# Transposing h and h2 by 32x32 blocks on VectorE, with DMAs inside SBUF that put the blocks in place

## The chip, the core and the metric

The kernel runs on one core of one Trainium2 chip. The metric is the device time in microseconds (us) of one execution. The kernel before was timed in three runs, and their median is what a changed kernel is held against. A profile is one more execution, taken by the hardware profiler, with a time and a span of its own.

## The reference, cut to what matters

Two layers work on a batch of 128 graphs, each with 128 nodes and 512 features. All data is float32.

```python
# x: [128, 128, 512], adj: [128, 128, 128]
# layer 0
h = relu(layernorm(x))
Xw = h @ Wv + bv
e  = leaky_relu(sj[:, None, :] + si[:, :, None] + ab)     # sj, si: Xw times the halves of aw
T  = adj * exp(e), each row divided by its sum
H  = sum over k = 0, 1, 2 of  (T^k h) @ Wk[k] + bk[k]
x  = x + relu(H)
# layer 1
h2 = relu(layernorm(x))
q, k = split(h2 @ Wqk);  v = h2 @ Wv1
w  = sum over d of q * (adj @ (k * mask)), scaled
x  = x + softmax(w over the nodes) * v
```

A product with a weight matrix needs the features of h on the partitions, since TensorE contracts over partitions. But h is computed with the nodes on the partitions. So h (for layer 0, the k = 0 term) and h2 (for layer 1) have to be transposed.

## The kernel before, in words

The 128 graphs are taken in 64 pairs (`G = 2`). A pair p passes through these steps, each of which is a function or a few lines:

- `load(p)` (L65 to L70) loads x and adj of a pair: two DMAs of SP's queue into `xg` and `ag`, with three buffers each.
- `norm0(p)` (L222) starts the load of pair p+1, if it wasn't started yet, normalizes x into `h` (`norm_relu`: statistics on VectorE, the last step L216 on ScalarE) and makes the two score columns from h with four VectorE operations (L231), whose full-size result `junk` is never read.
- `begin(p)` (L413) takes a tile `x` that will hold h, Th and T²h of the pair, transposed, and calls `transposed` for h.
- `transposed` (L234 to L240) transposes a pair's h: 8 TensorE transposes of 128x128, four into each of two PSUM tiles `pt` (L239), and then one copy of 128x512 from PSUM to SBUF on ScalarE and one on VectorE (L240).
- `attention(p)` and `t_transposed(p)` make T, T transposed and T² transposed; `propagate(p)` (L285) makes Th and T²h, transposed, with 16 TensorE instructions (L293) and four ScalarE copies (L295).
- `prepare0(p)` (L319) makes four sums of blocks of `x` on VectorE (`left_sums`, L301 to L304, 128x768 each), as Strassen's scheme with seven products wants them.
- `strassen0(p)` (L322) does layer 0's seven products (L313, 84 TensorE instructions of 256 columns), with VectorE additions between them (L332 to L347). A bank of PSUM takes a second product after VectorE has read the first: product 5 is added into the bank of product 6, once L335 has read that.
- `norm_relu` makes h2 of the pair. Its tile has one buffer, and the matmul that reads the h2 of the pair before (L383) has to be done first.
- a second call of `transposed` (L453) puts h2, transposed, into the tile `x2`, which has one buffer; L454 makes its four sums `sx2` (again L301 to L304, 128x256 each).
- `strassen1(p)` (L353) does layer 1's seven products (L313, 56 instructions of 512 columns), `aggregate(p)` the matmul with adj (L383) and a weighted sum (L386), `finish(p)` the softmax, the last addition (L409) and the store of the result (L411, SP's queue).

The loop at L427 overlaps neighbouring pairs: in round p stand `strassen0(p)`, with `begin` and `attention` of pair p+1 between its products, `propagate(p+1)`, `strassen1(p-1)`, `aggregate(p-1)`, `prepare0(p+1)`, `finish(p-1)`, the transposition of h2 of pair p with its sums, and `norm0(p+2)`.

The order in which an engine gets its instructions isn't the order of this text, though. The framework in which the kernel is written puts them in a queue for each engine at build time, by the order of the text and by when its own model of the machine finds them ready; it also writes the waits on semaphores. On the chip each queue runs strictly in order. So in the profile the statistics of `norm0(p+2)` stand ahead of `strassen1(p-1)`, and single instructions of `finish` lie between those of `norm0`. If an instruction isn't ready on the chip when its turn comes, all those behind it on its engine wait. DMAs take turns on eight semaphores; one that reads what DMAs wrote waits on each of the semaphores concerned. A wait that does not fit on an instruction is an instruction of its own (EVENT_SEMAPHORE).

Of the kernel before, what the change touches and what calls it, by code (L numbers as in the profile page):

```python
# [8 lines left out]
FP = mybir.dt.float32  # L9
# [6 lines left out]
def kernel(  # L16
# [20 lines left out]
    nc = tc.nc  # L37
    B, N, D = x.shape
    K = wk.shape[0]
    P = 128  # L40
    DC = D // P
    HC = DC // 2
    HD = D // 2
    G = 2
    NP = B // G
    EPS = 1e-5
    assert N == P and B <= P and B % G == 0 and D == 4 * P and K == 3
# [81 lines left out]
    ccol = setup.tile([P, 2], FP, name="ccol")  # L129
    for a in range(2):  # L130
        for c in range(DC):
            junk = front.tile([P, D], FP, name="junk")
            nc.vector.scalar_tensor_tensor(junk, wv0_sb[:, c, :], 1.0, aw_bc[:, a, :],
                                           op0=OP.mult, op1=OP.mult, accum_out=ucol[:, a, c:c + 1])
        pu = ps_t.tile([P, DC, P], FP, name="pt")
        for c in range(DC):
            spread(pu[:, c, :], ucol[:, a, c:c + 1])
        nc.vector.tensor_copy(u_bc[:, a, :], pu.rearrange("p c i -> p (c i)"))
        junk = front.tile([P, D], FP, name="junk")
        nc.vector.scalar_tensor_tensor(junk, bv_bc, 1.0, aw_bc[:, a, :],  # L140
                                       op0=OP.mult, op1=OP.mult, accum_out=ccol[:, a:a + 1])
    cz = const.tile([P, 1], FP, name="cz")
# [27 lines left out]
    right1 = {}  # L170
# [51 lines left out]
    def norm0(p):  # L222

        if p + 1 < NP and p + 1 not in xg:
            load(p + 1)
        h = H[p] = norm_relu(xg[p], "h", front)
        s = S[p] = small.tile([P, G, 2], FP, name="s")
        for j in range(G):
            for a in range(2):
                junk = front.tile([P, D], FP, name="junk")  # L230
                nc.vector.scalar_tensor_tensor(junk, h[:, j, :], 1.0, u_bc[:, a, :], op0=OP.mult,  # L231
                                               op1=OP.mult, accum_out=s[:, j, a:a + 1])

    def transposed(h, dst):  # L234

        for j in range(G):
            pt = ps_t.tile([P, 2, HC, P], FP, name="pt")
            for c in range(DC):
                nc.tensor.transpose(pt[:, c // HC, c % HC, :], h[:, j, c * P:(c + 1) * P], ident)  # L239
            (nc.vector.tensor_copy if j else nc.scalar.copy)(dst(j), pt)  # L240

    def attention(p):

# [41 lines left out]
    def propagate(p):  # L285

        h, tt = H.pop(p), TT.pop(p)
        for j in range(G):
            for kh in range(2):
                pt = ps_t.tile([P, HC, 2, N], FP, name="pt")  # L290
                for c in range(HC):
                    at = (kh * HC + c) * P
                    nc.tensor.matmul(pt[:, c].rearrange("p k n -> p (k n)"), h[:, j, at:at + P],  # L293
                                     tt[:, j].rearrange("p k n -> p (k n)"), start=True, stop=True)
                nc.scalar.copy(X[p][:, j, kh, 1:3].rearrange("p k c n -> p c k n"), pt)  # L295

    def left_sums(blocks, pool, name, width, bufs):

        s = pool.tile([P, 4, width], FP, name=name, bufs=bufs)
        a = [[blocks[:, j, kh] for kh in range(2)] for j in range(G)]  # L300
        nc.vector.tensor_add(s[:, 0], a[1][0], a[1][1])  # L301
        nc.vector.tensor_sub(s[:, 1], s[:, 0], a[0][0])  # L302
        nc.vector.tensor_sub(s[:, 2], a[0][0], a[1][0])
        nc.vector.tensor_sub(s[:, 3], a[0][1], s[:, 1])  # L304
        return dict(zip((5, 6, 7, 3, 1, 2, 4),
                        [s[:, 0], s[:, 1], s[:, 2], s[:, 3], a[0][0], a[0][1], a[1][1]]))

    def products(left, right, width):

        def product(bank, i, first):  # L310
            n = left[i].shape[1] // P
            for c in range(n):
                nc.tensor.matmul(bank[:, :width], left[i][:, c * P:(c + 1) * P], right[i][:, c],  # L313
                                 start=(first and c == 0), stop=(c == n - 1), skip_group_check=True)
        return product

    R0 = {i: t.rearrange("p k c o -> p (k c) o") for i, t in right0.items()}

    def prepare0(p):  # L319
        SX[p] = left_sums(X[p].rearrange("p j h k c n -> p j h (k c n)"), front, "sx", K * HD, 1)  # L320

    def strassen0(p, steps):  # L322

        product = products(SX.pop(p), R0, HD)
        X.pop(p)
        lo, hi = bsum[:, :HD], bsum[:, HD:]
        hb = X1[p] = front.tile([P, G, D], FP, name="x1", bufs=3)
        s = front.tile([P, 4, HD], FP, name="s0", bufs=1)
        ba, bb, bc = (ps_m.tile([P, D], FP, name="pm") for _ in range(3))
        a, b, c = ba[:, :HD], bb[:, :HD], bc[:, :HD]  # L330
        product(ba, 1, True)
        nc.vector.tensor_add(s[:, 0], a, hi)  # L332
        nc.vector.tensor_add(s[:, 1], a, lo)
        product(bb, 6, True)
        nc.vector.tensor_add(s[:, 2], b, s[:, 1])  # L335
        steps[0]()
# [12 lines left out]
        for j in range(G):  # L349
            nc.vector.scalar_tensor_tensor(hb[:, j, :], hb[:, j, :], 0.0, xs[:, j, :],  # L350
                                           op0=OP.max, op1=OP.add)

    def strassen1(p):  # L353

        product = products(SX2.pop(p), R1, D)
        X2.pop(p)
        yv = late["p"].tile([P, G, 2, 2, HD], FP, name="yv")
        o = [[yv[:, j, nh].rearrange("p k d -> p (k d)") for nh in range(2)] for j in range(G)]
        s = late["p"].tile([P, 3, D], FP, name="s1")
        a, b, c = (ps_m.tile([P, D], FP, name="pm") for _ in range(3))  # L360
        product(a, 1, True)
        nc.scalar.copy(s[:, 0], a)
        product(b, 6, True)
        nc.vector.tensor_add(s[:, 1], b, s[:, 0])
        product(c, 7, True)
        product(b, 5, False)
        nc.vector.tensor_add(s[:, 2], b, s[:, 0])
        nc.vector.tensor_add(o[1][1], c, s[:, 2])
        product(a, 2, False)
        nc.scalar.copy(o[0][0], a)  # L370
        product(b, 3, False)
        nc.vector.tensor_add(o[0][1], b, s[:, 0])  # L372
        product(c, 4, False)
        nc.vector.tensor_add(o[1][0], c, s[:, 1])  # L374
        return yv

    def aggregate(p, yv):

        h2, at = H2.pop(p), AT.pop(p)
        w = small.tile([P, 6, G], FP, name="w")  # L380
        for j in range(G):
            pa = ps_t.tile([P, D], FP, name="pt")
            nc.tensor.matmul(pa, at[:, j, :], h2[:, j, :], start=True, stop=True)  # L383
            junk = front.tile([P, D], FP, name="junk")
            b = p * G + j
            nc.vector.scalar_tensor_tensor(  # L386
                junk.rearrange("p (k d) -> p k d", k=2), pa.rearrange("p (k d) -> p k d", k=2),
                wscale[:, b:b + 1], yv[:, j, :, 0, :], op0=OP.mult, op1=OP.mult,
                accum_out=w[:, 0, j:j + 1])
        return w  # L390
# [20 lines left out]
        nc.sync.dma_start(out[p * G:(p + 1) * G].rearrange("b n d -> n b d"), x1)  # L411

    def begin(p):  # L413
        X[p] = front.tile([P, G, 2, K, HC, N], FP, name="x")
        transposed(H[p], lambda j: X[p][:, j, :, 0])

    nothing = (lambda: None, lambda: None)
    norm0(0)
# [6 lines left out]
    R1 = None  # L425
    W = {}
    for p in range(NP + 1):  # L427
# [9 lines left out]
        if p == 0:  # L437
            score_matrix()
            setup_ctx.close()
            R1 = {i: t.rearrange("p c k o -> p c (k o)") for i, t in right1.items()}  # L440
            late["p"] = ctx.enter_context(tc.tile_pool(name="late", bufs=1))
        if p < NP:
            H2[p] = norm_relu(X1[p], "h2", late["p"])
# [6 lines left out]
            finish(p - 1, yv, w)  # L450
        if p < NP:
            X2[p] = late["p"].tile([P, G, 2, HC, N], FP, name="x2")
            transposed(H2[p], lambda j: X2[p][:, j])  # L453
            SX2[p] = left_sums(X2[p].rearrange("p j h c n -> p j h (c n)"), late["p"], "sx2", HD, 1)  # L454
        if p + 2 < NP:
            norm0(p + 2)

# [24 lines left out]
```

## Time and profile before

| | |
|---|---|
| median of three runs | 2532.59 us (2530.12 to 2532.79) |
| the profiled execution | 2529.95 us, of which the span 2528.2 us |
| mean granted TensorE clock | 0.995 |
| busy: PE (matmul), PEld (weight load) | 2491.1 us, 1794.9 us |
| busy: DVE (VectorE), ACT (ScalarE) | 1700.4 us, 698.6 us |
| DMA moved | 86.28 MB in 62473 packets |
| one round in the steady state | 38.5 us |
| transposes of h and h2, L239 | 1024 instructions |
| copies of them to SBUF, L240 | 128 on ScalarE (586 ns each), 128 on VectorE (675 ns each) |

How to read it: the span is the time from the first to the last instruction of the profiled execution, and what the time has beyond it lies around the span. Busy times are sums over an engine's instructions in which overlaps count once. The engines run side by side, so that the busy times don't add up to the span. TensorE's matmuls overlap each other: the duration of one (273 ns for a transpose) is its latency, and the distance between two is what it costs TensorE.

### The profile page before, as it was taken

How to read it: one execution, taken by the hardware profiler on the slowest of the kernel's cores; microseconds unless marked ns; L12 is line 12 of the kernel's file. 1: busy time of each engine (PE TensorE's matmuls, PEld its weight loads, DVE VectorE, ACT ScalarE, POOL GpSimd, SP SyncE). 2: the span in 40 equal slices, each digit the busy share in tenths (PEclk: the TensorE clock that was granted, in tenths of full speed). 3: DMA queues.
4: the chain of work that ended last, by engine and by line, in shares of the span. 5: the costliest groups of instructions: out<-in, count | busy, mean ns of one | idle time of the engine just before them, and what ended most of it. 6: DMA issues, size and time to landing. Idle time of an engine off the chain costs nothing.

```text
span 2528.2 us, 28170 instructions
## 1 busy us (share of the span) xinstructions
PE 2491.1 (99%) x10313; PEld 1794.9 (71%) x10313; DVE 1700.4 (67%) x4648; ACT 698.6 (28%) x1677; POOL 0.7 (0%) x6
## 2 busy tenths in 40 slices
PE   5999999999999999999999999999999999999998
PEld 4677676776776776776767767767767767677675
DVE  6666667667667666666676676676666666766764
ACT  2322222223223223222222232232232222222321
POOL 0000000000000000000000000000000000000000
PEclk8999999999999999999999999999999999999999
DMA  5110010001000100100100010001001001000000
GB/s 161 36 38 30 28 38 29 29 30 36 30 30 28 38 30 28 38 30 28 38 28 30 30 36 30 30 28 38 30 28 38 30 27 36 30 30 30 34 9 25
DMA packets 62473, 86.28 MB, mean 34 GB/s; under 512 B 3712, under 2 KB 28416, under 8 KB 62336
## 3 DMA queue, kind: packets, MB, share of 16 engines
q1 hardware_dynamic: 62336, 84.49, 10.1%
q8 instruction: 81, 1.33, 0.2%
q14 instruction: 56, 0.46, 0.1%
HBM read 50.92 MB, written 33.55 MB: 33 GB/s over the span
## 4 chain that ended last, share of the span: by engine, by line
PE 96%; issue 0%; DVE 0%; ACT 0%; DVEq 0%; ACTq 0%
PE pm L313 75%; PE pt L293 8%; PE pt L239 4%; PE pt L383 4%; PE pt L124 1%; PE pt L281 1%; PE pt L277 1%; PE pt L266 1%; ACT h L216 0%; DVE junk L386 0%; DVE x L409 0%; ACT ej L400 0%; DVE yv L374 0%; DVEq L478 0%; DVE w L397 0%
## 5 line engine op out<-in xcount | busy, mean ns | idle before, releaser
L313 PE MATMUL pm<-t,sx 128*128 128x256 f32 x2304 | 518.6, 379 | 0.1
L313 PEld LDWEIGHTS pm<-t,sx 128*128 128x128 f32 x2304 | 432.6, 190 | 56.4 <-DVE sx L302 0.3
L313 PE MATMUL pm<-b,x 128*128 128x256 f32 x1536 | 390.8, 380 | 0.0
L313 PE MATMUL pm<-f,sx 128*128 128x512 f32 x768 | 340.1, 592 | 0.0
L313 PEld LDWEIGHTS pm<-b,x 128*128 128x128 f32 x1536 | 267.6, 191 | 55.2 <-issue 30.1
L295 ACT COPY x<-pt 128x512 f32<-128x512 f32 x256 | 147.6, 576 | 488.3 <-PE pt L293 488.3
L313 PEld LDWEIGHTS pm<-f,sx 128*128 128x128 f32 x768 | 145.6, 190 | 184.2 <-issue 150.2
L313 PE MATMUL pm<-e,x 128*128 128x512 f32 x512 | 240.6, 592 | 0.0
L293 PE MATMUL pt<-tt,h 128*128 128x256 f32 x1024 | 233.9, 382 | 0.5 <-ACT tt L282 0.5
L293 PEld LDWEIGHTS pt<-tt,h 128*128 128x128 f32 x1024 | 196.1, 192 | 27.9 <-ACT tt L282 0.8
L216 ACT ACTIVATE h<-x,rs 128x512 f32<-128x512 f32 x128 | 97.3, 807 | 290.1 <-PE pt L383 278.5
L313 PE MATMUL pm<-b,sx 128*128 128x256 f32 x768 | 176.2, 379 | 0.0
L313 PE MATMUL pm<-t,x 128*128 128x256 f32 x768 | 176.2, 379 | 0.0
L231 DVE SCALAR_TENSOR_TENSOR junk<-h,u_bc 128x512 f32<-128x512 f32 x256 | 174.4, 684 | 1.8 <-ACT h L216 1.8
L313 PEld LDWEIGHTS pm<-e,x 128*128 128x128 f32 x512 | 97.3, 190 | 95.6 <-issue 92.1
L313 PEld LDWEIGHTS pm<-b,sx 128*128 128x128 f32 x768 | 145.9, 190 | 19.8
L313 PEld LDWEIGHTS pm<-t,x 128*128 128x128 f32 x768 | 145.9, 190 | 19.8
L216 ACT ACTIVATE h<-xg,rs 128x512 f32<-128x512 f32 x128 | 97.1, 806 | 175.3 <-DVE rs L213 175.3
L239 PE MATMUL pt<-ident,h 128*128 128x128 f32 x1024 | 144.7, 274 | 0.7 <-ACT h L216 0.5
L240 ACT COPY x<-pt 128x512 f32<-128x512 f32 x128 | 75.1, 586 | 248.1 <-PE pt L239 242.3
L239 PEld LDWEIGHTS pt<-ident,h 128*128 128x128 f32 x1024 | 122.6, 142 | 14.1 <-ACT h L216 1.4
L372 DVE TENSOR_TENSOR yv<-pm,s 128x512 f32<-128x512 f32 x64 | 44.3, 692 | 129.0 <-PE pm L313 129.0
(105 smaller groups left out, 2844.9 us busy)
## 6 DMA issues: line engine op xcount, KB each, us to landing
xg<-in_x_dram SPq DMA_DIRECT2D x64, 512.0 KB, 3.5
out_dram<-x SPq DMA_DIRECT2D x64, 512.0 KB, 2.8
ag<-in_adj_dram SPq DMA_DIRECT2D x64, 128.0 KB, 2.1
b<-in_L_gnn_Wk_dram SPq DMA_DIRECT2D x12, 256.0 KB, 5.9
w<-in_L_gnn_Wqk_dram SPq DMA_DIRECT2D x8, 256.0 KB, 5.3
wv_sb<-in_L_gnn_Wv_dram SPq DMA_DIRECT2D x1, 1024.0 KB, 7.5
e<-in_L_gnn_Wv_dram SPq DMA_DIRECT2D x4, 256.0 KB, 6.1
bk_bc<-in_L_gnn_bk_dram SPq DMA_DIRECT2D x3, 256.0 KB, 5.8
```

The source lines that it names most:

```text
L124: nc.tensor.transpose(dst, col.to_broadcast([P, P]), ident)
L216: nc.scalar.activation(h[:, j, :], src[:, j, :], AF.Relu, bias=rs[:, 1, j:j + 1], scale=rs[:, 0, j:j + 1])
L231: nc.vector.scalar_tensor_tensor(junk, h[:, j, :], 1.0, u_bc[:, a, :], op0=OP.mult, op1=OP.mult, accum_out=s[:, j, a:a + 1])
L239: nc.tensor.transpose(pt[:, c // HC, c % HC, :], h[:, j, c * P:(c + 1) * P], ident)
L240: (nc.vector.tensor_copy if j else nc.scalar.copy)(dst(j), pt)
L266: nc.tensor.transpose(pa[:, j, :], a[:, j, :], ident)
L277: nc.tensor.transpose(pt[:, j, :], t[:, j, :], ident)
L293: nc.tensor.matmul(pt[:, c].rearrange("p k n -> p (k n)"), h[:, j, at:at + P], tt[:, j].rearrange("p k n -> p (k n)"), start=True, stop=True)
L295: nc.scalar.copy(X[p][:, j, kh, 1:3].rearrange("p k c n -> p c k n"), pt)
L313: nc.tensor.matmul(bank[:, :width], left[i][:, c * P:(c + 1) * P], right[i][:, c], start=(first and c == 0), stop=(c == n - 1), skip_group ...
L372: nc.vector.tensor_add(o[0][1], b, s[:, 0])
L383: nc.tensor.matmul(pa, at[:, j, :], h2[:, j, :], start=True, stop=True)
```

## The change

`transposed` no longer uses TensorE and PSUM. VectorE's `transpose` turns each 32x32 block of a tile within its place; two instructions do that for a pair, from `h` into a new tile `hv` with one buffer. Then every block still has to move to its own group of 32 partitions: 16 DMAs of SP's queue do that. DMA (n, f) takes the 32 partitions of nodes group n and, of each of 8 runs of 128 features (2 graphs x 4), the 32 columns of group f. It writes them to the 32 partitions of feature group f. So each of the 16 moves 32 partitions x 8 pieces of 32 float32, 128 bytes a piece and 32 KB in all. This is done for h in `begin`, and for h2.

The tile `x` gets another order of its dimensions, so that the DMAs can see it as 8 runs; `left_sums`, `products` and the names of the weights follow it, with the same numbers of instructions and the same shapes. The tile `junk` gets one buffer instead of two.

```diff
+    S32 = 32
+    Q = P // S32
...
-                junk = front.tile([P, D], FP, name="junk")
+                junk = front.tile([P, D], FP, name="junk", bufs=1)
...
     def transposed(h, dst):
 
-        for j in range(G):
-            pt = ps_t.tile([P, 2, HC, P], FP, name="pt")
-            for c in range(DC):
-                nc.tensor.transpose(pt[:, c // HC, c % HC, :], h[:, j, c * P:(c + 1) * P], ident)
-            (nc.vector.tensor_copy if j else nc.scalar.copy)(dst(j), pt)
+
+        hv = front.tile([P, G, D], FP, name="hv", bufs=1)
+        for j in range(G):
+            nc.vector.transpose(hv[:, j, :], h[:, j, :])
+        v = hv.rearrange("p g (c f b) -> p f (g c) b", f=Q, b=S32)
+        for n in range(Q):
+            for f in range(Q):
+                nc.sync.dma_start(dst[f * S32:(f + 1) * S32, :, n * S32:(n + 1) * S32],
+                                  v[n * S32:(n + 1) * S32, f])
...
-                nc.scalar.copy(X[p][:, j, kh, 1:3].rearrange("p k c n -> p c k n"), pt)
+                nc.scalar.copy(X[p][:, 1:3, j, kh].rearrange("p k c n -> p c k n"), pt)
...
     def begin(p):
-        X[p] = front.tile([P, G, 2, K, HC, N], FP, name="x")
-        transposed(H[p], lambda j: X[p][:, j, :, 0])
+        X[p] = front.tile([P, K, G, 2, HC, N], FP, name="x")
+        transposed(H[p], X[p][:, 0].rearrange("p j h c n -> p (j h c) n"))
...
             X2[p] = late["p"].tile([P, G, 2, HC, N], FP, name="x2")
-            transposed(H2[p], lambda j: X2[p][:, j])
-            SX2[p] = left_sums(X2[p].rearrange("p j h c n -> p j h (c n)"), late["p"], "sx2", HD, 1)
+            transposed(H2[p], X2[p].rearrange("p j h c n -> p (j h c) n"))
+            a = {(j, kh): X2[p][:, j, kh:kh + 1].rearrange("p k c n -> p k (c n)")
+                 for j in range(G) for kh in range(2)}
+            SX2[p] = left_sums(a, late["p"], "sx2", [1, HD])
```

More of the change, by code (lines that the diff above doesn't have):

```diff
@@ L138 @@
         nc.vector.tensor_copy(u_bc[:, a, :], pu.rearrange("p c i -> p (c i)"))
-        junk = front.tile([P, D], FP, name="junk")
+        junk = front.tile([P, D], FP, name="junk", bufs=1)
         nc.vector.scalar_tensor_tensor(junk, bv_bc, 1.0, aw_bc[:, a, :],
@@ L229, in norm0 @@
             for a in range(2):
-                junk = front.tile([P, D], FP, name="junk")
+                junk = front.tile([P, D], FP, name="junk", bufs=1)
                 nc.vector.scalar_tensor_tensor(junk, h[:, j, :], 1.0, u_bc[:, a, :], op0=OP.mult,
@@ L294, in propagate @@
                                      tt[:, j].rearrange("p k n -> p (k n)"), start=True, stop=True)
-                nc.scalar.copy(X[p][:, j, kh, 1:3].rearrange("p k c n -> p c k n"), pt)
[L297 to L304, printed above, removed]
+                nc.scalar.copy(X[p][:, 1:3, j, kh].rearrange("p k c n -> p c k n"), pt)
@@ L305, in left_sums @@
+    def left_sums(a, pool, name, width):
+        s = pool.tile([P, 4] + width, FP, name=name, bufs=1)
+        nc.vector.tensor_add(s[:, 0], a[1, 0], a[1, 1])
+        nc.vector.tensor_sub(s[:, 1], s[:, 0], a[0, 0])
+        nc.vector.tensor_sub(s[:, 2], a[0, 0], a[1, 0])
+        nc.vector.tensor_sub(s[:, 3], a[0, 1], s[:, 1])
         return dict(zip((5, 6, 7, 3, 1, 2, 4),
-                        [s[:, 0], s[:, 1], s[:, 2], s[:, 3], a[0][0], a[0][1], a[1][1]]))
-    def products(left, right, width):
+                        [s[:, 0], s[:, 1], s[:, 2], s[:, 3], a[0, 0], a[0, 1], a[1, 1]]))
@@ L310, in product, with products @@
+    def products(left, right):
         def product(bank, i, first):
[L311 to L314, printed above, removed]
+            _, n, m = left[i].shape
+            chunks = [(k, c) for k in range(n) for c in range(m // P)]
+            for at, (k, c) in enumerate(chunks):
+                r = right[i][:, k, c]
+                nc.tensor.matmul(bank[:, :r.shape[-1]], left[i][:, k, c * P:(c + 1) * P], r,
+                                 start=(first and at == 0), stop=(at == len(chunks) - 1),
+                                 skip_group_check=True)
@@ L315, in products @@
         return product
-    R0 = {i: t.rearrange("p k c o -> p (k c) o") for i, t in right0.items()}
     def prepare0(p):
-        SX[p] = left_sums(X[p].rearrange("p j h k c n -> p j h (k c n)"), front, "sx", K * HD, 1)
+        a = {(j, kh): X[p][:, :, j, kh].rearrange("p k c n -> p k (c n)")
+             for j in range(G) for kh in range(2)}
+        SX[p] = left_sums(a, front, "sx", [K, HD])
     def strassen0(p, steps):
-        product = products(SX.pop(p), R0, HD)
+        product = products(SX.pop(p), right0)
@@ L353, in strassen1 @@
     def strassen1(p):
-        product = products(SX2.pop(p), R1, D)
+        product = products(SX2.pop(p), R1)
         X2.pop(p)
@@ L383, in aggregate @@
             nc.tensor.matmul(pa, at[:, j, :], h2[:, j, :], start=True, stop=True)
-            junk = front.tile([P, D], FP, name="junk")
+            junk = front.tile([P, D], FP, name="junk", bufs=1)
             b = p * G + j
@@ L439 @@
             setup_ctx.close()
-            R1 = {i: t.rearrange("p c k o -> p c (k o)") for i, t in right1.items()}
+            R1 = {i: t.rearrange("p (s c) k o -> p s c (k o)", s=1) for i, t in right1.items()}
             late["p"] = ctx.enter_context(tc.tile_pool(name="late", bufs=1))
@@ L452 @@
             X2[p] = late["p"].tile([P, G, 2, HC, N], FP, name="x2")
-            transposed(H2[p], lambda j: X2[p][:, j])
-            SX2[p] = left_sums(X2[p].rearrange("p j h c n -> p j h (c n)"), late["p"], "sx2", HD, 1)
+            transposed(H2[p], X2[p].rearrange("p j h c n -> p (j h c) n"))
+            a = {(j, kh): X2[p][:, j, kh:kh + 1].rearrange("p k c n -> p k (c n)")
+                 for j in range(G) for kh in range(2)}
+            SX2[p] = left_sums(a, late["p"], "sx2", [1, HD])
         if p + 2 < NP:
```

## The prediction

> **What bounds the kernel now.** I read first the busy times (part 1 of the page), then the chain of work that ended last (part 4), then one round of that chain in order of time.
>
> ```profile
> PE 2491.1 (99%) x10313; PEld 1794.9 (71%) x10313; DVE 1700.4 (67%) x4648; ACT 698.6 (28%) x1677; POOL 0.7 (0%) x6
> PE 96%; issue 0%; DVE 0%; ACT 0%; DVEq 0%; ACTq 0%
> ```
>
> TensorE is busy for 99% of the span, and 96% of the chain is TensorE's own work: nothing but TensorE sets the pace, and a TensorE instruction that goes is worth its distance to the next one. The chain in order of time, for one steady round (columns: start, length, what):
>
> ```profile
> 1315.94 0.11 PE pt L124
> 1316.05 0.43 PE pm L313 x2
> 1316.48 0.20 PE pt L124
> 1316.68 0.44 PE pt L239 x4
> 1317.12 0.43 PE pm L313 x2
> 1317.55 0.44 PE pt L239 x4
> 1317.99 3.89 PE pm L313 x18
> 1321.88 0.87 PE pt L239 x8
> ```
>
> The 16 transposes of a round (8 of h2, 8 of h) take 0.44 + 0.44 + 0.87 = 1.75 us of the chain. A round is 38.5 us. The three stretches of that round show where the other engines have room (columns: stretch and its length, then the busy us of PE, PEld, DVE, ACT, POOL):
>
> ```profile
> 1299.50:1315.30 15.80, 15.80 (x43) 7.93 (x42) 10.54 (x27) 5.25 (x12) 0.00 (x0) 1.00 0.13 33
> 1315.30:1328.00 12.70, 12.70 (x71) 11.06 (x70) 11.24 (x38) 4.54 (x12) 0.00 (x0) 1.00 0.15 52
> 1328.00:1338.00 10.00, 10.00 (x51) 8.84 (x50) 4.38 (x9) 1.04 (x3) 0.00 (x0) 1.00 0.00 1
> ```
>
> All 16 transposes lie in the middle stretch, and there VectorE is 89% busy too (11.24 of 12.7). In the two others it has 5.3 and 5.6 us to spare.
>
> **What the Trainium skill says.** "VectorE: DVE Perf Modes", section on the three transpose paths, gives TensorE 390 ns and VectorE 311 ns for 128x128 in bf16, and says that VectorE does 32x32 blocks only. "TensorE: Matmul & The Clock Gate", Part 4, has 275 ns for a transpose inside a kernel: the trace has 273, but 109 ns from one to the next, which is what counts here. "DMA: Bandwidth & Descriptors" asks in its specifications for pieces of 512 B or more and says in its section on small descriptors that SBUF to SBUF is spared the penalty. No transfer of 128 B, and none inside SBUF, is in the trace of before. The packet records of that trace, sorted by size, have medians of 9 ns for 4 B, 27 ns for 512 B and 84 ns for 2 KB.
>
> **Part by part, for a round.**
>
> 1. Removed from TensorE: 16 transposes, 1.75 us, all of it on the chain. 64 x 1.75 = 112 us. The page agrees: L239 has "4%" of the chain, 88 to 114 us.
>
> 2. Removed copies (L240): two of 586 ns on ScalarE, two of 675 ns on VectorE. They lay beside TensorE's work: nothing on the chain.
>
> 3. Added on VectorE: four transposes of 128x512. The trace has none. From below, the copies they replace (0.67 us); from above, twice that, if four bytes take two passes. I take 0.69 us, so VectorE gains 4 x 0.69 - 2 x 0.675 = 1.4 us. The two for h can run in the first stretch, where h is ready at 1308.4 (ScalarE's L216 ends there) and VectorE is idle at times. The two for h2 take the place of the two copies in the middle stretch.
>
> 4. Added on SP: 32 DMAs. What one costs in SP's queue is seen at the start of the run, where seven follow each other without a wait (start, length):
>
> ```profile
> 0.74 0.43 SPq L68 DMA_DIRECT2D xg<-in_x_dram  x1
> 1.23 0.46 SPq L70 DMA_DIRECT2D ag<-in_adj_dram  x1
> 1.74 0.46 SPq L80 DMA_DIRECT2D aw_bc<-in_L_gnn_aw_dram  x1
> 2.24 0.43 SPq L82 DMA_DIRECT2D wv_sb<-in_L_gnn_Wv_dram  x1
> 2.72 0.50 SPq L84 DMA_DIRECT2D bv_bc<-in_L_gnn_bv_dram  x1
> ```
>
> They are 0.5 us apart, so 16 take 8 us, and SP is taken for 17 us of a round with its three other DMAs. Landing of the last: adj's 128 KB land 2.1 us after issue, so a whole transposition takes T = 10 us. The engines' part: each of 16 engines has 16 pieces of 128 B per DMA; on a line between 9 ns (4 B) and 27 ns (512 B) a piece takes 13.5 ns, 0.22 us per DMA, less than SP's 0.5. So the issue sets the pace.
>
> What hides T? h: ready at 1308.4, needed by `prepare0` at 1340.2: 30 us. h2: ready at 1317.1 (L216 ends), transposed at 1317.8, landed at 1327.8, needed by TensorE at 1340.1 (1338.4 in the shorter round): 10 us to spare. With the one buffer `hv`, if h goes first, from 1308.4 to about 1320, h2 follows to 1331, still 7 us early. So TensorE need not wait for either in the steady state. If T were 17 us, that cover would be gone.
>
> 5. Added waits. A reader of x and of x2 now waits for DMAs on eight semaphores rather than for two engines. The line of the transposes shows the price of one wait instruction:
>
> ```profile
> L239 PEldq EVENT_SEMAPHORE  x66: 51/51/81, 14.9 to 2504.1; - x66
> ```
>
> Six more, twice a round, are 0.61 us on TensorE's queue if none is hidden, 0 if the queue runs ahead. I take half: 0.3 us, 64 x 0.3 = 20 us. VectorE has them too, in front of its sums and of its transposes (about 1.2 us).
>
> 6. VectorE's crowding. Without the transposes the middle stretch is 10.95 us long. VectorE's work there: 11.24, less two copies (1.35), plus two transposes (1.38), less the sums of x2 (1.35) if they move behind the landing, plus about 0.8 of waits: 10.7 us. That fits by a hair. One buffer of `junk` instead of two may add a wait between six VectorE operations, up to 0.1 us each. TensorE loses between 0 and the whole 1.75 us; I take 0.3 us, 19 us in all.
>
> 7. The ends. At the start x isn't needed whole before 42 us, and h is there at 9: nothing. At the end TensorE has nothing else to do: h2 of the last pair is ready at 2504.75, and its products begin at 2506.15. They would begin at 2504.75 + 0.7 + 10 = 2515.5, less the matmuls L383 that fit into the gap: 8 us.
>
> Other edits (the order of the dimensions of x) keep shapes and counts: nothing.
>
> Sum on the profiled execution: 2528.2 - 112 + 20 + 19 + 8 = 2463.2 us of span, plus 1.75 around it = 2465. Its own time (2529.95) is 2.6 below the median, so 2468.
>
> **The rivals.**
>
> - Slower: VectorE's queue is blocked by the sums of x2. They are earlier in the program than the additions of the next pair's `strassen0`, so the order made at build time puts them at the moment when its model has the DMAs land. If that is before L335 (1323.8), VectorE stands at the sums until 1327.8, then does four sums (1.35) and L335 (0.4), and only then can product 5 start, at 1329.6 instead of 1325.8 - 1.75 = 1324.0: 5.6 us a round, 358 us, 2468 - 19 + 358 = 2807. It decides from a model that has 16 DMAs land in less than some 5 us. For it: in the first microseconds TensorE's queue has L124, which needs the load of Wv, ahead of L239, though h was ready first and L124 waited 10.7 us, so the model thought that load faster than it was. Against it: then several loads shared the bandwidth, here it is issue. If the sums stand behind L335 and the attention instead, the wait falls into the last stretch, where VectorE has 5.6 us free. 25 in 100, with part of the loss in some of it.
> - Slower: pieces of 128 B are slow. 512 a round and engine, beside 4.0 us of other transfers (10.1% of 2528 us over 64), fill the round from (36.75 - 4.0) / 512 = 64 ns a piece; at 80 ns a round is 45 us, 2880 us in all. Against it: 27 ns for 512 B. 10 in 100.
> - Little changes: VectorE takes back the whole gain in the middle stretch, by transposes of twice the length or by waits: 2528.2 - 112 + 20 + 112 + 8, about 2560 in the median, or 2530 where the waits are hidden. 12 in 100.
> - The change doesn't do what it says: excluded by the text, since no TensorE instruction is left in `transposed`.
>
> **How the numbers follow.** The forecast has 53 in 100: 2468, on its own 2425 (points 5 and 6 at nothing) to 2520. The slower cases range from 2540 to 2880. The range of 2424 to 2730 leaves out about 3 in 100 below and 15 above. A measurement of this kernel can tell 0.2%, 5 us, from no change. Faster by more than that: the 53 and a third of the third rival, 57 in 100; within it 5; slower 38.
>
> **What would show it.** No L239; a round of 37 to 37.4 us; SP's DMAs 0.4 to 0.5 us apart; landing about 2 us; VectorE's transposes near 0.69 us; L301 to L304 of x2 behind L335 and without a wait over 2 us. I am wrong if TensorE's weight loads wait for L335 or L339 by microseconds in every round (the first rival), or if DMA engines are busy over 90% (the second).

## The result, and the profile after

| | before | after |
|---|---|---|
| median | 2531.8 us (2530.12 to 2532.79, 4 runs) | 2550.52 us (2550.02 to 2551.03, 4 runs) |
| ratio, with its 95% interval | | 1.0075 (1.0057 to 1.0092) |
| span of the profiled execution | 2528.2 us | 2548.1 us |
| mean granted TensorE clock | 0.995 | 0.996 |
| one steady round | 38.49 us | 38.59 us |
| bytes moved by DMA | 86.28 MB | 153.60 MB |

The changed kernel is slower by 0.75%, 18.7 us. I had forecast 2468 us. A round here is the time from the first matmul with adj of one pair to that of the next (L383 before, L391 after); all rounds below are measured that way.

The line numbers have moved: the products are L320 (L313 before), the matmul with adj L391 (L383), its weighted sum L394 (L386), the spread of a column L126 (L124), h's last step L218 (L216), the four sums L306 to L309 (L301 to L304). VectorE's transposes are L241, the DMAs that place the blocks L245.

From the page after, the busy times and the chain that ended last:

```profile
PE 2446.3 (96%) x9289; PEld 1687.4 (66%) x9289; DVE 1799.1 (71%) x4776; ACT 666.3 (26%) x1549; POOL 0.7 (0%) x6
PE 91%; DVE 5%; issue 1%; DMA 1%; SPq 1%; ACT 0%; DVEq 0%; ACTq 0%
```

The 1024 transposes are gone from PE (10313 to 9289), but only 45 us of its busy time, and PE's share of the chain fell from 96% to 91%. VectorE has 5% of it, where it had nothing. The chain of one round in order of time says where (start, length, what):

```profile
1305.14 12.02 PE pm L320 x28
1317.16 0.87 PE pt L391 x2
...
1318.12 0.77 DVE junk L394 x2
...
1318.99 0.77 DVE junk L394 x2
...
1319.81 0.32 PE pt L126
...
1320.23 2.83 PE pm L320 x12
```

(The 28 instructions that begin at 1305.14 are layer 1's products of one pair; "56" above is twice as many as there are.) In the round of before that the prediction shows, two instructions of a product (L313) lie ahead of each L124 and cover the two VectorE operations that it waits for. Here TensorE's queue has L126 directly behind L391. The chain goes by way of VectorE, so that its two L391 are those of the first graph only; the timeline has TensorE at work on the second graph's up to 1318.88:

```profile
1317.00 1.88 PE L391 MATMUL pt<-h,aT 128*128 128x512 f32 x4
...
1318.94 0.32 PE L126 MATMUL pt<-ident,w 128*128 128x128 f32 x1
...
1319.81 0.32 PE L126 MATMUL pt<-ident,w 128*128 128x128 f32 x1 [0.55 <-DVE junk L394]
...
1320.23 2.83 PE L320 MATMUL pm<-b,x 128*128 128x256 f32 x12
```

So TensorE waits for L394 in every round. Over the whole run the list of waits has this line, where the kernel before has one such wait, of 1.3 us:

```profile
PE pt L126 <- DVE junk L394: 33.8, 60, 1.3
```

And behind the second L126 stand four wait instructions for the DMAs that wrote x. They are granted as soon as they are reached, but each takes its time, and L320 starts 0.42 us after that L126 in place of the 0.11 of two neighbours (`--source L320`, 1318.9 to 1320.4 us):

```profile
L320 PEldq EVENT_SEMAPHORE  x4: 51/51/51, 1319.8 to 1320.1; - x4
```

Where the whole loss lies can be read from the distances of TensorE's instructions. The fastest kernel below has rounds of 36.94 us, 1.65 less. Held against its rounds, the stretch from L391 to this L320 costs 1.20 us more, of which 0.3 are the four wait instructions. The other 0.45 lie behind the two later L126, where the products wait for VectorE (L307, one of `prepare0`'s sums, and L341). (Medians of 55 steady rounds; they hardly differ from round to round.)

Why the products had gone from between L391 and L126 is the question of the experiments. The next view is the timeline of after around it, those lines that have to do with `hv` (start, length, engine, line, what):

```profile
1304.52 0.70 DVE L241 STREAM_TRANSPOSE hv<-h 128x512 f32<-128x512 f32 x1
...
1306.18 20.87 SPq L245 DMA_DIRECT2D x<-hv  x18
...
1309.85 1.52 ACT L218 ACTIVATE h<-xg,rs 128x512 f32<-128x512 f32 x2 [1.49 <-DVE rs L215]
...
1318.91 1.52 ACT L218 ACTIVATE h<-x,rs 128x512 f32<-128x512 f32 x2 [4.57 <-PE pt L391]
...
1320.41 0.95 DVE L306 TENSOR_TENSOR sx<-x 128x768 f32<-128x768 f32 x1
...
1324.39 0.69 DVE L241 STREAM_TRANSPOSE hv<-h 128x512 f32<-128x512 f32 x1
```

The L218 lines are h (from xg) and h2 (from x); `x18` are h's 16 DMAs and the next two of h2. The transposition at 1304.52 is that of the h made a round earlier. The h of this round is ready at 1309.85 + 1.52, but the next transposition, at 1324.39, is that of h2, which was made 9 us later. h gets `hv` only after h2's 16 DMAs have landed, at 1304.52 + 38.59 = 1343.1: 33 us after its making began. In the round shown h's DMAs run from 1306.18 to 1316.9, and the last lands 2 us after its issue, at 1318.1. So `prepare0`'s first sum on the new x is at 1320.41, behind the matmul with adj and in the crowded middle stretch (before: at 1301.75, 12 us ahead of that matmul), and the first product that reads x is at 1320.23.

### The profile page after: what moved, and what is told of

Read it like the earlier page. It is cut to its first block, busy times and chain, and to the rows that moved or that the text cites. A ratio compares the mean times of both kernels' runs of the same rounds, so it can differ in the third digit from the quotient of the medians.

```text
span 2548.1 us, 29373 instructions
## 1 busy us (share of the span) xinstructions
PE 2446.3 (96%) x9289; PEld 1687.4 (66%) x9289; DVE 1799.1 (71%) x4776; ACT 666.3 (26%) x1549; POOL 0.7 (0%) x6
## 2 busy tenths in 40 slices
DMA packets 619545, 153.60 MB, mean 60 GB/s; under 512 B 560768, under 2 KB 585472, under 8 KB 619392
## 3 DMA queue, kind: packets, MB, share of 16 engines
q1 hardware_dynamic: 619392, 151.73, 27.4%
## 4 chain that ended last, share of the span: by engine, by line
PE 91%; DVE 5%; issue 1%; DMA 1%; SPq 1%; ACT 0%; DVEq 0%; ACTq 0%
PE pm L320 76%; PE pt L299 8%; DVE junk L394 4%; PE pt L391 2%; PE pt L126 1%; PE pt L287 1%; PE pm L190 1%; SPq L245 1%; PE pt L283 1%; PE pt L272 1%; DMA b<-in_L_gnn_Wk_dram 1%; DMA aw_bc<-in_L_gnn_aw_dram 0%; DVE sx L308 0%; DVE sx L306 0%; DVE sx L307 0%
## 5 line engine op out<-in xcount | busy, mean ns | idle before, releaser
L320 PE MATMUL pm<-t,sx 128*128 128x256 f32 x2304 | 532.6, 381 | 6.6 <-DVE sx L307 2.6
L320 PEld LDWEIGHTS pm<-t,sx 128*128 128x128 f32 x2304 | 427.7, 190 | 79.4 <-issue 23.7
L320 PE MATMUL pm<-b,x 128*128 128x256 f32 x1536 | 384.2, 386 | 6.5 <-DVE s L341 0.2
L320 PE MATMUL pm<-f,sx 128*128 128x512 f32 x768 | 340.9, 593 | 0.9 <-DVE sx L307 0.9
L320 PEld LDWEIGHTS pm<-b,x 128*128 128x128 f32 x1536 | 272.0, 190 | 56.8 <-issue 16.9
L320 PEld LDWEIGHTS pm<-f,sx 128*128 128x128 f32 x768 | 146.0, 190 | 186.2 <-issue 140.2
L301 ACT COPY x<-pt 128x512 f32<-128x512 f32 x256 | 149.8, 585 | 440.5 <-PE pt L299 440.5
L320 PE MATMUL pm<-e,x 128*128 128x512 f32 x512 | 242.5, 596 | 11.2 <-DMA x<-hv 11.2
L241 DVE STREAM_TRANSPOSE hv<-h 128x512 f32<-128x512 f32 x256 | 176.6, 699 | 1.8 <-ACT h L218 1.8
L320 PE MATMUL pm<-b,sx 128*128 128x256 f32 x768 | 176.5, 379 | 0.0
L320 PE MATMUL pm<-t,x 128*128 128x256 f32 x768 | 176.2, 379 | 0.0
L218 ACT ACTIVATE h<-x,rs 128x512 f32<-128x512 f32 x128 | 97.2, 806 | 287.0 <-PE pt L391 278.6
L320 PEld LDWEIGHTS pm<-e,x 128*128 128x128 f32 x512 | 97.7, 191 | 107.7 <-issue 90.9
L320 PEld LDWEIGHTS pm<-t,x 128*128 128x128 f32 x768 | 145.9, 190 | 19.8
L320 PEld LDWEIGHTS pm<-b,sx 128*128 128x128 f32 x768 | 145.6, 190 | 19.8
L375 DVE TENSOR_TENSOR s<-pm,s 128x512 f32<-128x512 f32 x64 | 44.3, 692 | 142.8 <-PE pm L320 142.8
L353 DVE TENSOR_TENSOR x<-pm,s 128x256 f32<-128x256 f32 x64 | 27.2, 425 | 139.7 <-PE pm L320 139.7
L218 ACT ACTIVATE h<-xg,rs 128x512 f32<-128x512 f32 x128 | 97.2, 806 | 96.3 <-DVE rs L215 96.3
```

Source lines behind the costliest of these rows:

```text
L218: nc.scalar.activation(h[:, j, :], src[:, j, :], AF.Relu, bias=rs[:, 1, j:j + 1], scale=rs[:, 0, j:j + 1])
L241: nc.vector.transpose(hv[:, j, :], h[:, j, :])
L301: nc.scalar.copy(X[p][:, 1:3, j, kh].rearrange("p k c n -> p c k n"), pt)
L320: nc.tensor.matmul(bank[:, :r.shape[-1]], left[i][:, k, c * P:(c + 1) * P], r, start=(first and at == 0), stop=(at == len(chunks) - 1), sk ...
```

## The experiments

Three theories were to be told apart.

- A: the one buffer `hv`. h waits for its turn with it; x is late; in the order made at build time the first products of `strassen0` then stand behind L126, and `prepare0`'s sums come to lie in the middle stretch.
- B: VectorE has too much to do in the middle stretch, whatever `hv` does (transposes, and sums behind the landing).
- C: the waits on eight semaphores cost TensorE's or VectorE's queue.

### Two buffers, one for h and one for h2

```diff
-    def transposed(h, dst):
-        hv = front.tile([P, G, D], FP, name="hv", bufs=1)
+    def transposed(h, dst, pool, name):
+        hv = pool.tile([P, G, D], FP, name=name, bufs=1)
...
-        transposed(H[p], X[p][:, 0]...)
+        transposed(H[p], X[p][:, 0]..., front, "hv")
...
-            transposed(H2[p], X2[p]...)
+            transposed(H2[p], X2[p]..., late["p"], "hw")
```

> The changed kernel with a second intermediate tile: h goes through hv as now, h2 through a tile of its own of the same size; nothing else differs. Theory A (the one buffer hv makes h wait for the DMAs of h2; x then lands just before its use, VectorE's four large sums and the wait of the spread of w fall where TensorE had other work): VectorE transposes h within about 2 us after ScalarE has made it, L306 to L309 with 768 columns run ahead of L375, the 1.5 us of L394 vanish from each round of the chain, a round is 36.8 to 37.2 us, the time is 2535 - 64 x 1.5 to 2550 - 64 x 1.7, that is 2440 to 2465 us. Theory B (VectorE is crowded by the four transposes and the waits on DMAs, whatever the buffers): the round stays at 38.4 us or more, 2530 us or more. Theory C (the waits on eight semaphores eat the gain on TensorE's queue): 38 us or more a round, 2520 us or more.

Measured: 2470.25 us (2467.33 to 2471.28), ratio 0.9755 (0.9741 to 0.977). This one buffer, and nothing else of the change, is worth 80 us. The chain of one round of it:

```profile
1314.39 1.72 PE pt L391 x4
1316.10 0.43 PE pm L320 x2
1316.54 0.11 PE pt L126
1316.64 0.43 PE pm L320 x2
1317.08 0.28 PE pt L126
```

The products are between L391 and L126 again, and TensorE doesn't wait. h is transposed at 1309.01, 0.85 us after L218 began, and `prepare0`'s sums run from 1302.63, ahead of the crowded stretch.

A round takes 37.27 us on average, though, and one in three takes 37.59. The chain of such a long one passes VectorE:

```profile
1366.03 4.33 PE pm L320 x20
...
1372.67 0.43 DVE sx L306
1373.10 0.34 DVE sx L308
1373.43 0.34 DVE sx L307
...
1383.31 1.42 DVE hv L241 x2
```

The three middle lines are sums of x2. They stand between the statistics of the norms, VectorE works with hardly a pause, and what follows on it, through h's transposes, is late. That is B in a small form, and the last experiments take it up.

### One buffer, h first

`norm0(p + 2)` and `begin(p + 2)` are moved ahead of h2's transposition in the loop, so that h has its turn with the one `hv` before h2.

```diff
+    begin(1)
     for p in range(NP + 1):
...
-                steps = (lambda: (begin(n), attention(n)), lambda: t_transposed(n))
+                steps = (lambda: attention(n), lambda: t_transposed(n))
...
         if p < NP:
+            if p + 2 < NP:
+                norm0(p + 2)
+                begin(p + 2)
             X2[p] = late["p"].tile([P, G, 2, HC, N], FP, name="x2")
...
-        if p + 2 < NP:
-            norm0(p + 2)
```

> The changed kernel, one hv as it is, with the turns exchanged: norm0 of pair p+2 and begin of pair p+2 stand ahead of the transposition of h2 of pair p in the program, so that h has hv first in every round. Same numbers of instructions, DMAs and buffers. Theory A, in the form that it is the turn and not the number of buffers that costs: h is transposed as soon as it is made, x lands some 25 us before its use, and the time is 2440 to 2480 us; h2 comes second, about 12 us later than in e1, which is still ahead of its use. Theories B and C: no change, 2530 us or more.

Measured: 2529.3 us (2524.47 to 2532.4), ratio 0.9989 (0.9982 to 0.9996). That is far from A's 2440 to 2480; by the number alone the run would speak for B or C. The timeline shows that the turn is exchanged, and so is the wait:

```profile
1299.21 1.52 ACT L218 ACTIVATE h<-x,rs 128x512 f32<-128x512 f32 x2 [3.41 <-DVE rs L214]
...
1303.43 10.39 SPq L245 DMA_DIRECT2D x<-hv  x16
...
1317.70 1.30 DVE L241 STREAM_TRANSPOSE hv<-h 128x512 f32<-128x512 f32 x2
```

Now h goes at once, and h2 (L218 with x), made from 1299.21, is transposed at 1317.70, after h's 16 DMAs. From one pair to the next it is 24.8 and 51.4 us in turn, and in the long ones TensorE's weight loads wait for x2's sums instead of for L394: 72.9 us in 32 waits, none over 2.8 us. One thing is mixed in: the load of xg is issued in the moved `norm0`, and in the long rounds the chain has 3.7 to 3.9 us of it. So the run shows that either order makes one of the two late; it doesn't show the price of that alone.

### The layout alone

Here TensorE transposes both again, into the new layout of x, and `junk` keeps its one buffer. Into the changed kernel comes a function that the next experiments use too:

```diff
+    def transposed_pe(h, dst):
+        d = dst.rearrange("p (j k c) n -> p j k c n", j=G, k=2)
+        for j in range(G):
+            pt = ps_t.tile([P, 2, HC, P], FP, name="pt")
+            for c in range(DC):
+                nc.tensor.transpose(pt[:, c // HC, c % HC, :], h[:, j, c * P:(c + 1) * P], ident)
+            (nc.vector.tensor_copy if j else nc.scalar.copy)(d[:, j], pt)
...
-        transposed(H[p], X[p][:, 0]...)
+        transposed_pe(H[p], X[p][:, 0]...)
...
-            transposed(H2[p], X2[p]...)
+            transposed_pe(H2[p], X2[p]...)
```

> The changed kernel with TensorE's transposes and their copies from PSUM put back, in the changed layout of x and with one buffer of junk: what is left of the change is the layout and junk. All theories of the transposition: as the kernel before, 2532 us within 0.2%, a round of 38.5 us. Were it 2540 or more, the layout or junk would be part of the loss.

Measured: 2537.61 us (2536.41 to 2538.77), ratio 1.0024 (1.0015 to 1.0033); a round takes 38.575 us, 0.085 more than before. In the chain the second L126 is 0.28 long,

```profile
1320.74 0.28 PE pt L126
```

and with two buffers of `junk`, in the layout otherwise the same,

```diff
-                junk = front.tile([P, D], FP, name="junk", bufs=1)
+                junk = front.tile([P, D], FP, name="junk")
```

> The layout of x and x2 of the changed kernel with TensorE's transposes, and two buffers of junk as before the change. If the 5.8 us that the layout alone with one buffer of junk is slower are the second product of L394 waiting for the first, this is 2532, the time before the change (2529 to 2535). If they are the layout, it stays at 2537.

it is 0.20 again:

```profile
1318.22 0.20 PE pt L126
```

Measured: 2531.83 us (2529.85 to 2532.29), ratio 1.0002 (0.9993 to 1.001). So the layout costs nothing that shows, and one buffer of `junk` costs 5.8 us: the second L394 starts 0.87 us after the first in place of 0.79, and the chain feels it once a round.

### h2 alone, and h alone

Only one of the two goes by blocks and DMAs, the other by `transposed_pe`. `hv` then has one user, and VectorE half of the added work. For h2 alone only the call in `begin` is changed back, for h alone only the one for h2.

> Only h2 goes through VectorE and DMAs, h through TensorE and PSUM as in the kernel before; hv then has one user. Theory A: TensorE loses 8 transposes a round, 0.87 us, without a new wait in the rounds; at the end the last pair waits for its DMAs, 9 to 12 us more; 2532 - 55 + 11, that is 2480 to 2495 us. Theory B: half of the crowding stays, 2515 us or more. Theory C: 2510 us or more.

Measured: 2495.94 us (2495.0 to 2496.92), ratio 0.9857 (0.9841 to 0.9874); a round takes 37.70 us.

> Only h is transposed by blocks and DMAs; h2 goes through TensorE and PSUM as before the change. hv then has one user. Theory A (h waits 33 us for hv because h2 has it): no one else has hv, so h is transposed right after ScalarE makes it, near 1308, and the whole of its 8 transposes is gained: 2537.6 (the layout alone) less 64 x 0.87 = 56, about 2482, between 2475 and 2490, and the last products don't wait, since h2 of the last pair doesn't go by DMA. Theory B (VectorE has too much to do in the middle stretch): half of the added work, so half of the loss stays, 2500 or more. Theory C (waits on eight semaphores cost TensorE): the same half, 2500 or more.

Measured: 2483.9 us (2482.89 to 2485.05), ratio 0.9813 (0.9796 to 0.9829); a round takes 37.70 us.

Each half gains 0.87 us a round against the layout alone (38.575), which is the whole of its eight transposes, to the hundredth. The difference of 12 us between the two is at the end: with h2 alone TensorE waits 12.3 us for the last DMAs, with h alone not at all. Together they lose what each gains alone; what they share is `hv`, VectorE's middle stretch and SP.

### Four DMAs in place of 16

```diff
-        v = hv.rearrange("p g (c f b) -> p f (g c) b", f=Q, b=S32)
+        v = hv.rearrange("p g (c b) -> p (g c) b", b=P)
         for n in range(Q):
-            for f in range(Q):
-                nc.sync.dma_start(dst[f * S32:(f + 1) * S32, :, n * S32:(n + 1) * S32],
-                                  v[n * S32:(n + 1) * S32, f])
+            nc.sync.dma_start(dst[n * S32:(n + 1) * S32], v[n * S32:(n + 1) * S32])
```

> The changed kernel, with one hv, but each transposition moves its bytes with 4 DMAs of pieces of 512 B instead of 16 DMAs of pieces of 128 B. This leaves out that a block changes its group of partitions: x and x2 are not the transposed tiles, all else has the same shapes and counts. Theory A: a transposition takes 4 x 0.65 + 2 = 4.6 us instead of 12, so h2 gives hv back some 7 us sooner, h follows inside the same round well ahead of prepare0, and VectorE's and TensorE's order has h's products early again: 2450 to 2475, without a second buffer. Theory B (VectorE's own work is the bound): VectorE does the same transposes and sums, so 2530 or more. Theory C: one DMA less in four to wait for, a part of it back, 2500 to 2530.

Measured: 2442.37 us (2441.42 to 2442.66), ratio 0.9647 (0.9632 to 0.9661). The pieces in its trace are of 4 KB, 16384 of them, not of 512 B. The rounds are 36.94 us with one `hv` and all of VectorE's transposes and sums (DVE is busy for 1774.9 us, after for 1799.1). That excludes B as the cause of the loss: VectorE's own work fits. It was faster than A's range for it.

### One buffer, the DMAs on two queues

The run before has bigger and fewer pieces too, and its blocks stay in their partitions. So here every second DMA of the changed kernel is issued by ScalarE, and nothing else differs.

```diff
-                nc.sync.dma_start(dst[f * S32:(f + 1) * S32, :, n * S32:(n + 1) * S32],
+                (nc.sync if f % 2 else nc.scalar).dma_start(dst[f * S32:...
```

> The changed kernel with its one hv, its 16 DMAs of 128-byte pieces and the right result, but every second DMA is issued from ScalarE's queue, the others from SP's. Theory A: a transposition is over after 8 x 0.65 + 2 = 7.2 us instead of 12, h2 gives hv back 5 us sooner, and h follows in the same round; TensorE's order has h's first products ahead of the two L126 again. 2445 to 2490, the end's wait for the last DMAs shorter than 11 us. If the size of the pieces was what the run with 4 DMAs removed, and not the time for which hv is held, nothing is gained: 2535 or more. Against a gain also: ScalarE issues 16 DMAs a round, 10 us if one takes it as long as SP, and its copies free PSUM: if they come late, 2500 to 2550.

Measured: 2456.27 us (2455.31 to 2458.87), ratio 0.9704 (0.9689 to 0.9718). The timeline of a round:

```profile
1310.37 0.71 DVE L241 STREAM_TRANSPOSE hv<-h 128x512 f32<-128x512 f32 x1
...
1312.24 6.05 ACTq L245 DMA_DIRECT2D x<-hv  x8
1315.52 3.24 SPq L245 DMA_DIRECT2D x<-hv  x4
...
1322.67 0.70 DVE L241 STREAM_TRANSPOSE hv<-h 128x512 f32<-128x512 f32 x1
...
1324.34 5.23 ACTq L245 DMA_DIRECT2D x<-hv  x8
```

h2 has its turn from 1310.37, h from 1322.67: still in the order of the text, but h follows 12.3 us behind h2, where the changed kernel has 18.7 (1324.39 to 1343.1), and its DMAs are issued in 5.5 us in place of 10.7. Its x is there before `prepare0`'s sums at 1332.84. Two in three rounds take 36.94 us. Same pieces, same number of DMAs and semaphores, same buffers: so it is the length of a turn with `hv` that decides (A), not the size of the pieces, and not the waits (C). TensorE's queue has ten wait instructions in such a round, eleven in the changed kernel; the four for x stand among layer 1's products, where they cost nothing. The same edit on top of two buffers (below) is worth 13.5 us, so most of the 94 us here isn't the quicker landing by itself.

### A version that is faster than both

Two buffers, and TensorE's transposes at both ends of the run, where it has nothing else to do:

```diff
+        if p == 0:
+            transposed_pe(H[p], d)
+        else:
+            transposed(H[p], d, front, "hv")
...
+            if p == NP - 1:
+                transposed_pe(H2[p], d)
+            else:
+                transposed(H2[p], d, late["p"], "hw")
```

> Two buffers for the blocks (hv for h, hw for h2), and at both ends, where TensorE has nothing else to do, the transposes are TensorE's again: h of pair 0 and h2 of the last pair. Against two buffers alone (2470) the end should give back the wait of TensorE for the last DMAs, about 11 us in the changed kernel, and the start up to 2: 2457 to 2462. If the end's wait was cheap because something else ended late anyway, 2468 to 2471.

Measured: 2456.96 us (2456.34 to 2457.3), ratio 0.9705 (0.969 to 0.9719): 13.3 us less than with two buffers alone. To this, every second DMA from another queue, ScalarE's or GpSimd's:

```diff
-                nc.sync.dma_start(dst[f * S32:...
+                (nc.sync if f % 2 else nc.scalar).dma_start(dst[f * S32:...
```

> Two buffers and the ends by TensorE (2457), and every second DMA from ScalarE's queue. x2 is there 5 us sooner, so x2's sums no longer stand in VectorE's queue between the sums of the norms: the rounds of 37.6 go and all take about 36.8 to 36.95, the time of the run with 4 DMAs. 63 x (37.28 - 36.9) = 24 us: 2430 to 2440. If ScalarE's issuing delays its copies: 2457 to 2490.

Measured: 2443.51 us (2441.21 to 2444.07), ratio 0.965 (0.9635 to 0.9664). 43 of 61 rounds take 36.94 us, single ones up to 38.0. They were to go altogether, and the time is 3 us above what was expected. In most of the long rounds TensorE waits for the transposition of T. It hangs on the exponential of the attention, which stands in ScalarE's queue behind its DMAs: VectorE waits for it for 50.0 us in all, up to 2.2 at a time, in the next kernel for 30.3, up to 0.5.

> The same, with every second DMA from the queue of GpSimd, which does nothing else. If it issues a DMA as fast as SP (0.65 us): 2430 to 2440. If its DMAs take 1.3 us or more each, the halves from it land no sooner than all of them from SP, and it stays at 2457 or gets worse.

Measured: 2435.06 us (2433.27 to 2436.26), ratio 0.9616 (0.96 to 0.9632). All steady rounds take 36.94 us. It is the fastest of all the kernels run, 97 us below the kernel before. What its trace has for the DMAs of GpSimd (engine, what, count: shortest, median and longest in ns):

```profile
L245 POOL DMA_DIRECT2D x<-hv x504: 582/582/714, 40.3 to 2338.5; - x168
L245 POOL DMA_DIRECT2D x<-hw x504: 582/582/598, 93.5 to 2384.3; - x168
```

So GpSimd issues at least as fast as SP (609 ns).

## Why the prediction was wrong

The step that failed is in point 4: "With the one buffer `hv`, if h goes first, from 1308.4 to about 1320, h2 follows to 1331, still 7 us early". The "if" is denied by the text of the kernel. A buffer that two steps share is handed on in the order of the text. h of pair p+2 is made in round p but transposed by `begin`, which stands in `strassen0` of round p+1; the transposition of h2 of pair p is in round p, ahead of both. So h2 comes first, although h is ready 9 us earlier. In the profile before, the making of h2 (L216) begins at 1315.54. From there two turns of some 14 us each (transposes 1.4, issue 10.4, landing 2) would end at 1343.5 at the earliest, and x was needed at 1340.2. With the 10 us of point 4 the same order would by this sum (an estimate) have fitted by a hair: h2 landed at 1327.8, h 11.4 us later at 1339.2. So the order of the turns and the length of one failed together. In the changed kernel x is there 39.7 us after the matmul with adj of the round (1318.1 + 38.6 - 1317.0); before, it was read 26.6 us after it (1340.2 - 1313.6).

The conclusion of point 4, that TensorE need not wait for either, also asked only whether x lands ahead of its use. It does, by 2 us (1318.1 and 1320.2). What TensorE waits for is L394, since the products that had covered this wait now stand behind it. That they were put there because the model at build time has x land late is inferred: the queues show the order, not the model's reasons.

Turning the order around in the text only made h2 late (2529.3 us); two buffers (2470.25), one user (2495.94, 2483.9) or a shorter turn (2456.27, 2442.37) gave the gain back.

The other points, in their order:

1. 1.75 us a round off TensorE: right. Each half alone gains 0.87 us a round.
2. The copies cost nothing on the chain: nothing speaks against it. ScalarE is busy for 32 us less, and in both profiles it has 0% of the chain.
3. 0.69 us for a transpose: right, the mean of 256 is 699 ns. "VectorE: DVE Perf Modes" of the Trainium skill, section on the three transpose paths, has 311 ns for 128x128 in bf16; here four times as many elements of four bytes take 2.25 times that.
4. A landing of 2 us and 13.5 ns a piece were right: the trace has 2.0 us, and 13 ns as the median of 524288 records of 128 B. The issue was taken too short, 0.5 us from one to the next; it is 0.65 to 0.67:

```profile
L245 SPq DMA_DIRECT2D x<-hv x2048: 585/609/1838, 23.1 to 2522.4; - x187
```

   The seven DMAs at the start from which I took 0.5 us took 430 to 500 ns each in SP's queue; those of 32 partitions with 8 pieces take 609. So T is 12 us, not 10. With a buffer for each that costs little: 37.27 us a round where two queues (SP and GpSimd) give 36.94, some 20 us in 61 rounds.
5. and 6. Waits and crowding at 0.3 us each were too dear where `hv` isn't in the way: 36.94 is 0.20 above 38.49 - 1.75 = 36.74, and 0.085 of these are the one buffer of `junk`, which I had within its bound. In the changed kernel the same terms are 38.59 - 36.74 = 1.85, as a consequence of point 4; the waits on TensorE's queue have 0.3 of it, as forecast.
7. The end: 8 us forecast. TensorE's last wait is 11.2 us; in the groups by shape, before this was 0.0:

```profile
L320 PE MATMUL pm<-e,x 128*128 128x512 f32 x512 | 242.5, 596 | 11.2 <-DMA x<-hv 11.2
```

   The last h2 is transposed by 2504.5, but the first of its DMAs is issued at 2511.21. The tile `x2` has one buffer, and only then is TensorE through with the products of the pair before, which read it:

```profile
2509.30 1.88 PE L320 MATMUL pm<-f,x 128*128 128x512 f32 x4
```

   That is 6.7 us, and a second single buffer whose other user I hadn't looked at. Seven DMAs later the store of the pair before (L419) comes up in SP's queue and waits for the last addition (L417); the other nine are issued from 2517.00 on, 1.2 us later than at the distance of the others. I had named SP's queue as a place where others stand, and had not looked at who stands there at the end. From the matmul with adj that ends the steady rounds to the end of the span it is 73.1 us, before 59.9: 13.2 us more, where I had 8.

In the sum: the steady rounds are 38.58 - 37.34 = 1.24 us longer than forecast, 76 us over 61 rounds; three more rounds to which I had given the gain are at the ends, 3 us; the end is 5 us longer, the start 1 us. Together that is the 85 us by which the span exceeds 2463.2.

Of the rivals, the third, that VectorE takes back the whole gain in the middle stretch, came nearest in number (2560) and had the place right, but not the mechanism: the transposes aren't longer, and of the 1.65 us between 38.59 and 36.94 some 0.9 are waits for L394 that the order on TensorE has laid bare, 0.45 waits for a crowded VectorE (`prepare0`'s late sum L307, and L341), and 0.3 the wait instructions. The first rival, VectorE standing at the sums of x2 until they land, didn't happen: VectorE has one such wait in the whole run, of 8.0 us, at the end. The second didn't happen either: the DMA queue is busy for 27.4% of 16 engines' span.

By luck the forecast fits another kernel: with a buffer for each, the sum of the same terms is right to 3 us (2470.25 for 2468), the waits too dear and the issue too cheap by about as much.

## What to carry to other kernels

Before a new buffer is taken as free when its data are ready, write down who uses it in the order of the program's text, give each use its length (here transposes, issue of all DMAs, landing: 14 us), and see when the last one ends against its need; a use can wait for another one that becomes ready later. If it doesn't fit, try a second buffer (80 us here) or a shorter use (94 us, by the DMAs over two queues) first. And in an order that is made at build time, a late tile can also move what had covered other waits: look at which instructions lie between a wait and its cause, as the products between L391 and L126 do here.

## What the runs showed of the hardware

- A piece of 128 B inside SBUF takes 13 ns on a DMA engine in the median, one of 4 KB (the run with four DMAs) 315 ns. "DMA: Bandwidth & Descriptors" of the Trainium skill, section on small descriptors, says that SBUF to SBUF is spared the penalty for small ones; by these two numbers a byte costs 1.3 times as much in the small piece, so the trace agrees nearly. What little there is was hidden here: the issue (0.65 us for a DMA of 32 KB) set the pace. (The 27 ns for 512 B of the prediction are transfers from and to DRAM.)
- "SBUF — State Buffer" of the Trainium skill, section on the two separate sides, warns that DMAs of GpSimd's queue are held up while VectorE runs certain operations between SBUF and SBUF. No such case shows here: with VectorE busy for 74% of the span, the 1008 DMAs that GpSimd issued took 582 ns in the median and 714 at most. None of this shows that VectorE ran such an operation at the time.
- The DMAs of GpSimd's queue have 16 records of 2 KB each, besides records of 4 B, where those of SP's queue have 256 of 128 B. One of 2 KB takes 213 ns in the median, which is 13 ns for each of 16 pieces.
- A wait that is granted already isn't free where the queue has no lead: four of them, 51 ns each, hold up TensorE for 0.3 us a round behind L126. In the run with one buffer and two queues the group for x stands among layer 1's products, which are 0.43 us apart, and no gap shows.
